# A graph layer, a mixer and merged experts on one core: the head written out step by step, the weight merge shared with TensorE, the last norm divided anew

## The chip, the cores and the metric

The kernel runs on one core of a Trainium2 chip. The core has four engines that compute, TensorE (PE), VectorE (DVE), ScalarE (ACT) and GpSimd (POOL), and SyncE (SP), whose queue issues the DMAs here. Each engine works through its own queue in order and waits on semaphores for what others produce. The metric is device time in microseconds of one execution. Times that are read from the trace count from the first instruction of the span.

## The reference, cut to what matters

```python
xn = layernorm(x)                                  # x: 1250 x 512
h = prelu(xn @ lin_W.T + lin_b, lin_a)             # the linear layer of the head
for l in range(2):                                 # graph convolution
    h = h + segment_sum(h[src], dst)               # 41250 edges, sorted by dst
    h = prelu(h @ W1[l].T + b1[l], a[l]) @ W2[l].T + b2[l]
    h = relu(batchnorm(h))
x = x + h + mixer(xn)                              # linear attention, layer norm
y = layernorm(x)
g = (relu(y @ gfc1.T + b) @ gfc2.T + b2).mean(0)   # 8 gates, one set for all rows
W1m = W1 + sum(g[e] * tv_W1[e]);  b1m = b1 + g @ tv_b1
W2m = W2 + sum(g[e] * tv_W2[e]);  b2m = b2 + g @ tv_b2
out = x + norm(y + relu(y @ W1m.T + b1m) @ W2m.T + b2m)
```

## The kernel before

Nodes lie in ten tiles of 128 rows (the last has 98), features in four tiles of 128. A float32 product over four feature tiles appears in the trace as eight PE records.

**The head** (lines 694 to 864). For each row tile `x_first` takes mean and variance on VectorE and the root on ScalarE, `x_second` the inverse on VectorE and the normalised rows on ScalarE, `x_third` turns the rows by PE into features and copies them out of PSUM on ScalarE (line 607). `lin(c0, cn, f)` makes the product of one feature tile for `cn` nodes (PE, line 576), two Relu sides on ScalarE (612, 613), and their sum on VectorE (614). The node parts are 256, 256, 384 and 354 wide. Before the first rows arrive PE turns the identity 22 times (line 723). The calls stand under `given(engines={PE, DVE, Activation})`: on these three engines the order of the queue is the order of the program, up to `head.close()` at line 861. The last part of the linear layer, and all up to the second layer's end, is ordered by the framework's own planner; from line 1200 on the program's order holds again.

**The graph as a matrix.** Between these calls the lines 745 to 794 make, from the sorted edges, the first destination of each of the 81 blocks of 512 edges (`ends`, `span`, `base`), and keys (`s_hi`, `s_lo`, `key`). `weave(us)` then lets blocks into the work at a rate of 0.70 per microsecond given: for a block, one-hot rows `oh_s` and `oh_k` on VectorE (832, 834), or, for every third block, `oh_s` on ScalarE (817, 818); four PE products (849); and an add into `adj` (851). `drain(keep=2)` leaves two blocks between making and counting. 10 of the 81 blocks are let in during the linear layer, the others in the key stage (line 884) and after it. The first graph product (line 981) needs all.

**The merge** (lines 1300 to 1366). When the gates are known (line 1297), eight expert weights are added to `m1` (4 chunks of 128x256) and `m2` (2 chunks of 128x512). On VectorE: `m1` chunks 0, 1, 2 and `m2` chunk 0, each as a chain of eight multiply-adds in a PSUM bank. By ScalarE scaling in place and GpSimd adding: `m1` chunk 3 and `m2` chunk 1. `joined(c)` multiplies chunk `c` into six PSUM banks (`parts`: two feature tiles by three node parts, line 1325), and after chunk 3 ScalarE takes the Relu. The bias row `b2` is one product (1334) before chunk 0; it is added to the rows `xn2` in advance, tiles 0 to 4 on VectorE, 5 to 9 on GpSimd.

**The end** (lines 1370 to 1442). For each row tile: product (1374), sum with `xn2` on VectorE (1384, 1388), the norm, and the store. A `NEAR` tile has its last steps on VectorE (1413 to 1416), any other one on ScalarE and GpSimd (1424 to 1429). Tiles in `BY_SCALAR` have their variance taken on ScalarE, and their last steps three tiles later.

Of the kernel before, what the change touches and what calls it, by code (L numbers as in the profile page):

```python
# [9 lines left out]
F32 = mybir.dt.float32  # L10
# [515 lines left out]
def usual_block(  # L526
# [75 lines left out]
    def to_features(dst, t, src, n):  # L602

        pt = bank()
        for c in range(DT):
            nc.tensor.transpose(pt[:, c * P:c * P + n], src[:, c * P:(c + 1) * P], ident[0:n, 0:n])
        nc.scalar.copy(dst[:, :, t * P:t * P + n], pt.rearrange("p (c n) -> p c n", c=DT)[:, :, 0:n])  # L607

    def prelu(dst, ps, cn, bias, slope):

        u = tmp.tile([P, CHUNKS[0][1]], F32, tag="xt", bufs=4, name="u")
        nc.scalar.activation(dst, ps[:, :cn], AF.Relu, bias=v(*bias))  # L612
        nc.scalar.activation(u[:, :cn], ps[:, :cn], AF.Relu, bias=minus(*bias), scale=-1.0)  # L613
        nc.vector.scalar_tensor_tensor(dst, u[:, :cn], minus(*slope), dst, op0=ALU.mult, op1=ALU.add)  # L614
# [79 lines left out]
    x_live = {}  # L694

    def x_first(t):
        x_live[t] = spread(x_in[0:rows(t), t, :], rows(t))

    def x_second(t):
        n = rows(t)  # L700
        mv, rs = x_live.pop(t)
        inverse(mv, rs, n)
        normal(xn[0:n, t, :], x_in[0:n, t, :], rs, n)

    def x_third(t):
        to_features(xn_t, t, xn[0:rows(t), t, :], rows(t))

    h_t = large("C", [P, DT, N], name="h_t")

    def lin(c0, cn, f):  # L710
        ps = bank()
        gemm(ps, cn, lambda c: lw[:, c, f * P:(f + 1) * P], lambda c: xn_t[:, c, c0:c0 + cn])
        prelu(h_t[:, f, c0:c0 + cn], ps, cn, ("lin_b", f), ("lin_a", f))
# [3 lines left out]
    head = ExitStack()  # L717
    head.enter_context(given(engines={E.PE, E.DVE, E.Activation}))
    idle = bank()

    def stay_warm(n):
        for i in range(n):
            nc.tensor.transpose(idle[:, 0:P], ident, ident)

    stay_warm(22)
    x_first(0)
    x_first(1)
    x_second(0)
    x_second(1)
    x_third(0)  # L730
    x_third(1)
    stay_warm(3)
    x_first(2)
    x_second(2)
    x_first(3)
    x_second(3)
    lin(0, 256, 0)
    x_third(2)
    x_first(4)
    lin(0, 256, 1)  # L740
    x_third(3)
    x_second(4)
    x_first(5)
    lin(0, 256, 2)
    e_d = early.tile([P, NB, J], F32, name="e_d")
    nc.scalar.copy(e_d, edges[:, :, 1, :])
    ends = early.tile([P, 2, NB], F32, name="ends")
    nc.vector.tensor_reduce(ends[:, 0, :], e_d, AX.X, ALU.min)
    real = early.tile([P, NB, J], F32, name="real")
    nc.vector.scalar_tensor_tensor(real, e_d, float(N), e_d, op0=ALU.is_lt, op1=ALU.mult)  # L750
    nc.vector.tensor_reduce(ends[:, 1, :], real, AX.X, ALU.max)
    x_second(5)
    lin(0, 256, 3)
    x_third(4)
    x_first(6)
    pts = [bank(), bank()]
    lin(256, 256, 0)
    for k in range(2):
        nc.tensor.transpose(pts[k][0:NB, 0:P], ends[:, k, :], ident)
    span = early.tile([NB, 2], F32, name="span")  # L760
    for k, op in ((0, ALU.min), (1, ALU.max)):
        nc.vector.tensor_reduce(span[:, k:k + 1], pts[k][0:NB, 0:P], AX.X, op)
    x_second(6)

    s_hi = early.tile([P, NB, J], I32, name="s_hi")
    nc.vector.tensor_scalar(s_hi, edges[:, :, 0, :], 7, None, op0=ALU.logical_shift_right)
    lin(256, 256, 1)
    x_third(5)
    x_first(7)
    lows, highs = bank(), bank()  # L770
    nc.tensor.transpose(lows[:, 0:NB], span[:, 0:1].to_broadcast([NB, P]), ident[0:NB, 0:NB])
    nc.tensor.transpose(highs[:, 0:NB], span[:, 1:2].to_broadcast([NB, P]), ident[0:NB, 0:NB])
    base = const.tile([P, NB], F32, name="base")
    nc.vector.tensor_scalar(base, lows[:, 0:NB], float(N - W), None, op0=ALU.min)
    base_i = early.tile([1, NB], I32, name="base_i")
    nc.vector.tensor_copy(base_i, base[0:1, :])
    lin(256, 256, 2)
    x_third(6)
    x_second(7)
    low = const.tile([1, 2, NB], F32, name="low")  # L780
    nc.scalar.copy(low[:, 0, :], lows[0:1, 0:NB])
    nc.scalar.copy(low[:, 1, :], highs[0:1, 0:NB])
    key = e_d
    nc.vector.tensor_tensor(key, e_d, base.unsqueeze(2).to_broadcast([P, NB, J]), ALU.subtract)
    nc.vector.tensor_scalar(real, key, float(W), float(BIG), op0=ALU.is_ge, op1=ALU.mult)
    x_first(8)
    lin(256, 256, 3)
    nc.vector.tensor_tensor(key, key, real, ALU.add)
    nc.vector.scalar_tensor_tensor(key, s_hi, float(W), key, op0=ALU.mult, op1=ALU.add)
    x_second(8)  # L790
    x_first(9)
    lin(512, 384, 0)
    s_lo = early.tile([P, NB, J], F32, name="s_lo")
    nc.vector.scalar_tensor_tensor(s_lo, s_hi, -float(P), edges[:, :, 0, :], op0=ALU.mult, op1=ALU.add)
    x_third(7)
    x_second(9)
# [13 lines left out]

    held, state = [], {"block": 0, "due": 0.0, "at": []}

    def source_rows(b, oh_s):

        off = hot.tile([P, J, P], F16, bufs=2, name="off")
        for j in range(J):
            nc.scalar.activation(off[:, j, :], count16[:, 0:P], AF.Abs, bias=s_lo[:, b, j:j + 1], scale=-1.0)
        nc.scalar.activation(oh_s, off, AF.Relu, bias=1.0, scale=-1.0)  # L818

    def weave(us, keep=2):  # L820

        state["due"] += us * PACE
        while state["block"] < min(NB, state["due"]):
            b = state["block"]
            state["block"] += 1
            oh_s = hot.tile([P, J, P], F16, name="oh_s")
            oh_k = hot.tile([P, J, NT * W], F16, name="oh_k")
            if b % 3 == 1 and b > 3:
                source_rows(b, oh_s)
            for j in range(J):  # L830
                if b % 3 != 1 or b <= 3:
                    nc.vector.tensor_scalar(oh_s[:, j, :], count16[:, 0:P], s_lo[:, b, j:j + 1], None,  # L832
                                            op0=ALU.is_equal)
                nc.vector.tensor_scalar(oh_k[:, j, :], count16, key[:, b, j:j + 1], None, op0=ALU.is_equal)  # L834
            held.append((b, oh_s, oh_k))
            drain(keep)

    def drain(keep):
        while len(held) > keep:
            b, oh_s, oh_k = held.pop(0)  # L840
            if b % 16 == 0:
                k = min(16, NB - b)
                _, state["at"] = nc.values_load_multi_w_load_instructions(
                    base_i[0:1, b:b + k], engines=[mybir.EngineType.DVE], min_val=0, max_val=N - W,
                    skip_runtime_bounds_check_because="both ends are taken from 0 to N - W",
                )
            ps = bank()
            for j in range(J):
                nc.tensor.matmul(ps[:, 0:NT * W], oh_s[:, j, :], oh_k[:, j, :], start=(j == 0), stop=(j == J - 1))  # L849
            at = ds(state["at"][b % 16], W)  # L850
            nc.vector.tensor_tensor(adj_r[:, :, at], adj[:, :, at],  # L851
                                    ps[:, 0:NT * W].rearrange("p (s d) -> p s d", s=NT), ALU.add)

    PACE = 0.70

    for f in range(1, DT):
        weave(1.4)
        lin(512, 384, f)
        if f < 3:
            x_third(f + 7)  # L860
    head.close()
    for f in range(DT):
        weave(2.4)
        lin(896, 354, f)
# [433 lines left out]
    nc.scalar.activation(gate9[0:NE, :], pg9[0:NE, 0:P], AF.Identity, bias=g2bc, scale=1.0 / N)  # L1298
# [4 lines left out]
    parts = [(f, b, bank()) for f in range(FT) for b in range(len(CHUNKS))]  # L1303
# [5 lines left out]
    def merge(acc, dst, srcs, at, alone=False):  # L1309

        for e in range(0 if alone else 1, NE):
            nc.vector.scalar_tensor_tensor(dst[at] if alone and e == NE - 1 else acc, srcs[e][at], gate[:, e:e + 1],
                                           dst[at] if alone and e == 0 else acc, op0=ALU.mult, op1=ALU.add)
        if not alone:
            nc.vector.tensor_tensor(dst[at], acc, dst[at], ALU.add)

    def merge_far(dst, srcs, at):
        for e in range(NE):
            scaled(srcs[e][at], e, srcs[e][at])
            nc.gpsimd.tensor_tensor(dst[at], dst[at], srcs[e][at], ALU.add)  # L1320
# [190 lines left out]
```

## Time and profile before

| | |
|---|---|
| times of three runs | 571.64, 571.74, 572.16 us; median 571.74 |
| the profiled execution | 570.89 us, its span 569.1 us |
| mean granted PE clock | 0.989 |
| busy PE, DVE, ACT, POOL | 545.6, 324.7, 244.2, 75.3 us |
| first linear product starts | 8.41 us |
| first key product starts | 57.33 us |
| first graph product starts | 203.22 us |
| products of the gate layer end | 515.37 us |
| gates known | 517.22 us |
| joined products | 521.52 to 540.40 us |
| output products | 540.40 to 557.73 us |
| VectorE's last instruction ends | 563.17 us |

Busy time is the time in which an engine executes an instruction; a wait isn't in it. A record of the trace gives an instruction's start and duration. Where instructions of a kind follow one another without a wait, the distance of their starts is less than the duration, because the next begins while the last is finishing; a sum over many uses that distance, a wait for a result uses the duration. The profiled execution is one of several, and 0.85 us below the median.

### The profile page before, as it was taken

To read this page: it belongs to the slowest core of one execution; us is meant where nothing else is said; L and a number is where in the kernel's file an instruction comes from. 1 tells how busy PE (TensorE), PEld (TensorE's weight loads), DVE (VectorE), ACT (ScalarE), POOL (GpSimd) and SP (SyncE) were. 2 spreads that over 40 slices of the span, in tenths; PEclk is the share of its full clock that TensorE was granted. 3 is DMA by queue.
4 is the path that set the end of the run, shared out by engine and by line. 5 is a ranking of instruction groups with operands and counts; after the bars stand their busy time and mean duration, and the time that the engine had idled before them with its cause. 6 is when DMAs were issued, how large, how long until landed. Compare 5 with 4: busy or idle time off the path is not lost. (4 is left out here: it accounts for less than half of the span.)

```text
span 569.1 us, 6958 instructions
## 1 busy us (share of the span) xinstructions
PE 545.6 (96%) x2367; PEld 368.1 (65%) x2367; DVE 324.7 (57%) x1097; ACT 244.2 (43%) x539; POOL 75.3 (13%) x73
## 2 busy tenths in 40 slices
PE   8799999999999999999999999999999999997992
PEld 7655568799955567777754454449995556864540
DVE  4579999976899724444425534121112248726885
ACT  6676664554354212223333344112333446726453
POOL 8200000000000000000004331000000001204972
PEclk9999999999999999999999999999999999997997
DMA  9500200020021010000311102000008320402014
GB/s 282 184 1 1 74 2 1 1 75 2 1 94 56 0 75 0 1 1 2 104 44 37 37 1 74 0 0 1 2 0 282 124 74 1 147 1 75 0 41 146
DMA packets 19285, 29.10 MB, mean 51 GB/s; under 512 B 1529, under 2 KB 8185, under 8 KB 19240
## 3 DMA queue, kind: packets, MB, share of 16 engines
q1 hardware_dynamic: 19096, 28.52, 14.8%
q8 instruction: 20, 0.33, 0.2%
q14 instruction: 25, 0.20, 0.1%
q10 hardware_dynamic: 144, 0.05, 0.0%
HBM read 26.01 MB, written 2.56 MB: 50 GB/s over the span
## 5 line engine op out<-in xcount | busy, mean ns | idle before, releaser
L981 PE MATMUL bank<-adj,y_h 128*128 128x416 f32 (+1 forms) x240 | 86.5, 361 | 1.1 <-DVE adj L851 1.1
L834 DVE TENSOR_SCALAR oh_k<-count,e_d 128x240 f16<-128x240 f16 x324 | 84.4, 281 | 0.0
L981 PE MATMUL bank<-adj,y_l 128*128 128x416 f32 (+1 forms) x240 | 84.4, 352 | 0.0
L1083 POOL TENSOR_TENSOR m<-m,ls_bc 128x512 f32<-128x512 f32 (+1 forms) x10 | 12.7, 1270 | 447.6 <-ACT m L600 447.6
L968 PE MATMUL bank<-w,h_t 128*128 128x512 f32 (+1 forms) x160 | 70.4, 592 | 0.0
L576 PE MATMUL bank<-z_t,w 128*128 128x416 f32 (+1 forms) x192 | 68.9, 513 | 0.0
L576 PEld LDWEIGHTS bank<-z_t,w 128*128 128x128 f32 x192 | 36.1, 189 | 31.8 <-issue 30.0
L832 DVE TENSOR_SCALAR oh_s<-count,s_lo 128x128 f16<-128x128 f16 x220 | 55.8, 254 | 0.0
L968 PEld LDWEIGHTS bank<-w,h_t 128*128 128x128 f32 (+1 forms) x160 | 29.4, 188 | 34.8 <-issue 34.5
L614 DVE SCALAR_TENSOR_TENSOR z_t<-u,m_sb,z_t 128x416 f32<-128x416 f32 (+1 forms) x24 | 15.7, 652 | 59.8 <-ACT u L613 59.8
L981 PEld LDWEIGHTS bank<-adj,y_h 128*128 128x128 f32 x240 | 45.1, 188 | 2.6 <-issue 2.1
L981 PEld LDWEIGHTS bank<-adj,y_l 128*128 128x128 f32 x240 | 45.2, 188 | 1.2 <-issue 0.7
L849 PE MATMUL bank<-oh_k,oh_s 128*128 128x240 f16 x324 | 41.8, 266 | 1.6 <-ACT oh_s L818 1.2
L849 PEld LDWEIGHTS <-oh_s 128*128 128x128 f16 x324 | 31.6, 98 | 16.4 <-issue 5.3
L612 ACT ACTIVATE z_t<-bank,v_sb 128x416 f32<-128x416 f32 (+1 forms) x24 | 14.7, 610 | 61.4 <-PE bank L981 61.4
L851 DVE TENSOR_TENSOR adj<-adj,bank 128x240 f32 x81 | 32.7, 404 | 13.9 <-PE bank L849 12.5
L995 DVE BATCH_NORM_STATS2 bst<-bank 128x6 f32<-128x416 f32 (+1 forms) x24 | 14.4, 600 | 42.9 <-ACT h_t L994 42.9
L917 PE MATMUL bank<-kk,xn 128*128 128x128 f32 (+1 forms) x320 | 38.4, 275 | 0.0
L576 PE MATMUL bank<-xn_t,lw 128*128 128x256 f32 (+2 forms) x128 | 36.6, 428 | 0.8 <-ACT xn_t L607 0.8
L917 PEld LDWEIGHTS bank<-kk,xn 128*128 128x128 f32 (+1 forms) x320 | 37.0, 192 | 0.1
L1064 PE MATMUL bank<-mixer,q_t 128*128 128x512 f32 (+1 forms) x80 | 36.3, 592 | 0.0
L576 PE MATMUL bank<-xn_t,gw 128*128 128x256 f32 (+2 forms) x128 | 35.3, 427 | 0.9 <-ACT xn_t L607 0.9
(172 smaller groups left out, 797.3 us busy)
## 6 DMA issues: line engine op xcount, KB each, us to landing
t<-in_tv_w SPq DMA_DIRECT2D x12, 512.0 KB, 7.6
w<-in_conv_w SPq DMA_DIRECT2D x4, 1024.0 KB, 5.4
x_in<-in_x SPq DMA_DIRECT2D x9, 256.0 KB, 4.7
xt<-in_x SPq DMA_DIRECT2D x9, 256.0 KB, 4.2
out<-m SPq DMA_DIRECT2D x9, 256.0 KB, 2.7
rest<-in_tv_w SPq DMA_DIRECT2D x4, 512.0 KB, 5.1
lw<-in_lin_w SPq DMA_DIRECT2D x4, 256.0 KB, 5.1
wk<-in_w_qkv SPq DMA_DIRECT2D x1, 1024.0 KB, 7.1
```

Of the source, the lines that this page charges most:

```text
L576: nc.tensor.matmul(ps[:, :cn], lhs(c), rhs(c), start=(c == 0), stop=(c == k - 1))
L612: nc.scalar.activation(dst, ps[:, :cn], AF.Relu, bias=v(*bias))
L614: nc.vector.scalar_tensor_tensor(dst, u[:, :cn], minus(*slope), dst, op0=ALU.mult, op1=ALU.add)
L832: nc.vector.tensor_scalar(oh_s[:, j, :], count16[:, 0:P], s_lo[:, b, j:j + 1], None, op0=ALU.is_equal)
L834: nc.vector.tensor_scalar(oh_k[:, j, :], count16, key[:, b, j:j + 1], None, op0=ALU.is_equal)
L849: nc.tensor.matmul(ps[:, 0:NT * W], oh_s[:, j, :], oh_k[:, j, :], start=(j == 0), stop=(j == J - 1))
L851: nc.vector.tensor_tensor(adj_r[:, :, at], adj[:, :, at], ps[:, 0:NT * W].rearrange("p (s d) -> p s d", s=NT), ALU.add)
L917: nc.tensor.matmul(ps[:, c * P:(c + 1) * P], xn[0:n, t, c * P:(c + 1) * P], k_nodes(f)[0:n, t, :], start=(t == 0), stop=(t == NT - 1))
L968: nc.tensor.matmul(ps[:n], h_t[:, c, t * P:t * P + n], w1[:, c, :], start=(c == 0), stop=(c == DT - 1))
L981: nc.tensor.matmul(ps[:, :cn], y[0:n, s, f * P:(f + 1) * P], adj_r[0:n, s, c0:c0 + cn], start=(s == 0 and y is ys[0]), stop=(s == NT - 1 a ...
L995: nc.vector.bn_stats(st[:, b, :], ps[:, :cn])
L1064: nc.tensor.matmul(ps[:n], q_t[:, h, t * P:t * P + n], mixer[:, h, :], start=(h == 0), stop=(h == DT - 1))
```

## The change

Three places change. What each engine computes for the result is the same sum in another division.

1. **The head.** Each call is split into single steps of one engine, and the string `HEAD_ORDER` gives their order to the end of the linear layer; the digits are the tile, or part and feature tile. The node parts are 128, 256, 384 and 482. The copy of tile 0 is on VectorE. ScalarE makes one-hot rows only for blocks after the ninth. All ten blocks of the head are also counted and added within it.
2. **The merge.** In chunk 0 of `m1` the left 128 columns are summed by PE, with identities scaled by the gates as one operand; the right 128 stay on VectorE. Chunk 1 goes to ScalarE and GpSimd, chunks 2 and 3 to VectorE as one piece of 512 columns. The bias row's product and `gate9` come later. `joined` takes its parts in a given list; the last two parts of chunk 3 come before output tile 5. Row tiles 0 to 5 get their bias on VectorE.
3. **The last norm.** Tile 5 leaves `NEAR` and `BY_SCALAR`; the last steps of a `BY_SCALAR` tile come two tiles later instead of three.

```diff
+    HEAD_ORDER = """
+        s0 s1 q0 r0 q1 s2 n0 r1 t0 q2 s3 n1 c0 t1 q3 r3 m00 c1 r2 n2 m01 u00 n3 t2 j00 m02 s4 u01 c2 j01
+        t3 s5 u02 m03 ed j02 q5 m10 ends u03 q4 c3 j03 tends s6 u10 m11 r5 q6 span n5 r4 hi n4 tspan s8
+        m12 u11 base low key q8 t5 r8 u12 t4 put m13 c5 j12 c4 j10 n8 r6 lo m20 n6 s9 u13 s7 q9 j13 q7
+        j11 t6 r7 u20 m21 r9 b0 c6 n7 j20 n9 b1 d0 u21 m22 j21 b2 t7 u22 m23 b3 c7 b4 d1 u23 t9 j22 t8
+        c9 d2 j23 c8 d3 a0 b5 m30 b6 b7 d4 u30 m31 j30 a3 a4 a2 b8 d5 u31 m32 b9 j31 a5 d6 a1 u32 m33 a6
+        j32 d7 u33 d8 a7 d9 a8 j33 a9
+    """
+    PARTS = ((0, 128), (128, 256), (384, 384), (768, 482))
+    COPIED_BY_VECTOR = (0,)
...
+    def one_hot_rows(b):
...
+        by_scalar = b % 3 == 1 and b > 9
...
+    def counts(b):
+        _, oh_s, oh_k = held.pop(0)
+        live["block", b] = ps = bank()
+        for j in range(J):
+            nc.tensor.matmul(ps[:, 0:NT * W], oh_s[:, j, :], oh_k[:, j, :], start=(j == 0), stop=(j == J - 1))
...
+    STEPS = {
+        "s": x_stats, "q": x_root, "r": lambda t: inverse(x_mv[:, t, :], x_rs[:, t, :], rows(t)), "n": x_normal,
+        "t": x_turn, "c": x_copy, "m": lin_product, "u": lin_sides, "j": lin_join,
+        "ed": lambda: nc.scalar.copy(e_d, edges[:, :, 1, :]), "ends": ends_of_blocks, "tends": turn_ends,
+        "span": reduce_ends, "tspan": spread_ends, "base": bases, "low": lowest, "hi": source_high,
+        "lo": source_low, "key": keys_in_band, "put": keys, "b": one_hot_rows, "d": counts, "a": add_counts,
+    }
+    with given(engines={E.PE, E.DVE, E.Activation}):
...
+        for step in HEAD_ORDER.split():
+            name = step.rstrip("0123456789")
+            STEPS[name](*(int(i) for i in step[len(name):]))
...
+    state["due"] = float(state["block"])
...
-    nc.scalar.activation(gate9[0:NE, :], pg9[0:NE, 0:P], AF.Identity, bias=g2bc, scale=1.0 / N)
...
+    gated = [tmp.tile([P, 2, P], F32, tag="xt", bufs=4, name="gated") for _ in range(NE // 2)]
+    one = [flat(t, 1, 2) for t in t1s]
+    two = [flat(t, 2, 4) for t in t1s]
+    for e in (0, 1, 2, 4, 5, 6):
+        nc.vector.tensor_scalar(gated[e // 2][:, e % 2, :], ident, gate[:, e:e + 1], None, op0=ALU.mult)
+    scaled(gated[1][:, 1, :], 3, ident)
+    merge_far(flat(m1, 1, 2), one, [0])
+    scaled(gated[3][:, 1, :], 7, ident)
+    merge_far(flat(m1, 1, 2), one, [1, 2])
+    nc.tensor.matmul(sums[1][:, 0:P], ident, m1[:, 0, 0:P], start=True, stop=False)
     for e in range(NE):
+        nc.tensor.matmul(sums[1][:, 0:P], gated[e // 2][:, e % 2, :], t1s[e][:, 0, 0:P],
+                         start=False, stop=(e == NE - 1))
+    acc = sums[0][:, 0:FF - P]
+    for e in range(NE):
+        nc.vector.scalar_tensor_tensor(m1[:, 0, P:FF] if e == NE - 1 else acc, t1s[e][:, 0, P:FF], gate[:, e:e + 1],
+                                       m1[:, 0, P:FF] if e == 0 else acc, op0=ALU.mult, op1=ALU.add)
+    nc.scalar.copy(m1[:, 0, 0:P], sums[1][:, 0:P])
+    joined(0, sorted(parts, key=lambda p: p[0]))
+    merge_far(flat(m1, 1, 2), one, [3])
+    scaled(sums[1], 0, two[0])
+    merge_far(flat(m1, 1, 2), one, range(4, NE))
     nc.vector.tensor_reduce(mb1, mb, AX.X, ALU.add)
+    merge(sums[1], flat(m1, 2, 4), two)
...
+    nc.scalar.activation(gate9[0:NE, :], pg9[0:NE, 0:P], AF.Identity, bias=g2bc, scale=1.0 / N)
...
+    far2 = [t[:, 1, :] for t in t2s]
+    merge_far(m2[:, 1, :], far2, range(2))
+    joined(1, parts)
+    nc.tensor.matmul(sums[0], gate9, r9[:, 0, :], start=True, stop=True)
+    nc.scalar.copy(b2, sums[0])
+    shifted(0)
+    scaled(sums[1], 0, t2s[0][:, 0, :])
+    merge(sums[1], m2[:, 0, :], [t[:, 0, :] for t in t2s])
+    merge_far(m2[:, 1, :], far2, range(2, NE))
+    joined(2, parts)
+    joined(3, parts[0:4])
+    for t in range(1, NT):
+        shifted(t)
...
-    NEAR, BY_SCALAR = (4, 5, 7, 8, 9), (5, 7, 8, 9)
+    NEAR, BY_SCALAR = (4, 7, 8, 9), (7, 8, 9)
...
-    for t in range(NT + 3):
+    for t in range(NT + 2):
         for u in NEAR:
-            if u == t - (3 if u in BY_SCALAR else 1):
+            if u == t - (2 if u in BY_SCALAR else 1):
                 out_near(u)
+        if t == 5:
+            joined(3, parts[4:])
         if t < NT:
             out_product(t)
             out_sum(t)
```

The steps are: `s` statistics, `q` root, `r` inverse, `n` normalise, `t` turn, `c` copy, `m` product, `u` the two Relu sides, `j` their join, `b` one-hot rows of a block, `d` its counts, `a` the add into `adj`; the named ones are the edge preparation. `merge_far(dst, srcs, es)` now takes the experts as a list: ScalarE scales, GpSimd adds. `shifted(t)` adds the bias row to tile `t`, on VectorE for `t < 6`, else on GpSimd.

## The prediction

> **What bounds the kernel.** I read the page first, then PE's waits, then a table by stretches, then the timeline of the two places that the change touches. The page says how long, which engine, and at what clock:
>
> ```profile
> span 569.1 us, 6958 instructions
> PE 545.6 (96%) x2367; PEld 368.1 (65%) x2367; DVE 324.7 (57%) x1097; ACT 244.2 (43%) x539; POOL 75.3 (13%) x73
> PEclk9999999999999999999999999999999999997997
> ```
>
> TensorE is the bound: 96% busy, at full clock but for two slices near the end. So a gain is idle PE time taken out, or slow-clock time. Where it idled, from PE's waits (waiter, releaser, us in total, times, longest):
>
> ```profile
> PE bank L1325 <- DVE m L1312: 2.5, 1, 2.5
> PE bank L771 <- DVE span L762: 2.4, 1, 2.4
> PE bank L576 <- ACT xn_t L607: 1.7, 3, 0.9
> PE bank L849 <- ACT oh_s L818: 1.2, 1, 1.2
> PE bank L981 <- DVE adj L851: 1.1, 1, 1.1
> ```
>
> The first lies in the weight merge, the others but for the last mostly in the head. By stretches (start:end, length, busy us and instructions of PE, PEld, DVE, ACT, POOL; PE clock; DMA share; GB/s):
>
> ```profile
> 8.41:20.00 11.59, 11.06 (x57) 9.34 (x58) 6.34 (x20) 7.46 (x17) 8.84 (x11) 1.00 1.06 348
> 20.00:40.00 20.00, 17.03 (x77) 11.57 (x76) 12.65 (x44) 13.67 (x33) 0.00 (x0) 1.00 0.08 29
> 40.00:57.33 17.33, 15.78 (x74) 9.71 (x72) 16.04 (x75) 11.79 (x30) 0.00 (x0) 1.00 0.00 1
> 57.33:202.13 144.80, 144.80 (x862) 104.37 (x861) 125.23 (x594) 66.95 (x171) 0.00 (x0) 1.00 0.09 30
> 515.20:521.52 6.32, 3.34 (x19) 1.78 (x17) 4.34 (x11) 3.87 (x10) 1.70 (x4) 0.78 0.47 167
> 521.52:540.40 18.88, 18.88 (x49) 10.15 (x50) 16.42 (x30) 10.86 (x20) 17.94 (x18) 0.89 0.00 1
> ```
>
> From 57.33, the first key product (call it T), PE has no gap until 202. So time saved before T is saved at 202, if VectorE still feeds the one-hot blocks as early relative to T. Last, the timeline of the merge and the end (start, us, engine, line):
>
> ```profile
> 521.52 19.04 PE L1325 MATMUL bank<-xn_t,m 128*128 128x418 f32 x48 [2.54 <-DVE m L1312]
> 540.40 17.33 PE L1374 MATMUL bank<-m,a_t 128*128 128x512 f32 x40
> 562.42 0.75 DVE L1416 SCALAR_TENSOR_TENSOR m<-bank,rs,x_sb 98x512 f32<-98x512 f32 x1
> ```
>
> The end is VectorE's: it finishes 5.4 us after the last product, then a store.
>
> **The head: PE's work.** A product is eight PE records. From the timeline these start 0.216 us apart at 256 columns, 0.322 at 384, 0.297 at 354, 0.350 at 418, 0.429 at 512, 0.112 at 128. At 482 no row exists; between 418 and 512 it is 0.404. Before: 4 x 8 x (0.216 + 0.216 + 0.322 + 0.297) = 33.6 us. After (128, 256, 384, 482): 4 x 8 x (0.112 + 0.216 + 0.322 + 0.404) = 33.7. No work is saved. Besides, from the first product on: eight row turns of 0.435 = 3.5, the block ends some 0.8, ten blocks of counts at 0.41 = 4.1 (before 9.75 blocks by T). Sum after: 42.2. Before, T - 8.41 = 48.9 for 41.8 of work: 7.1 us of holes.
>
> **The head: does PE run dry?** I walk the written order, each engine taking its steps in sequence at the spacing of their rows: statistics 0.83, root 0.21 (result 0.30), inverse 0.27, normalise 0.71 (result 0.82), copy 0.48 (0.58), the two Relu sides 2 x 0.26, 0.36, 0.46, 0.54 (by width; the first and last along the line through the others), join 0.27, 0.40, 0.54, 0.64, one block's one-hot rows 1.42 on VectorE, count add 0.31; 0.04 from engine to engine. The same walk over the old order gives its first product at 8.38 (trace 8.41), the turned ends at 24.23 (24.28), the first product of 384 at 28.98 (29.19). It errs by 0.2.
>
> The new start is later. VectorE: s0 to 4.33, s1 to 5.16, r0 to 5.43, then s2, which waits until 6.67 for its rows; r1, now behind s2, ends 7.77 (before: 5.9). s3 waits for the fourth tile (issued 3.16, longest landing of this group 5.1: 8.26) and holds the copy c0 behind it; that copy on VectorE lies between ScalarE's 0.58 and the 0.70 of L1388, taken 0.65. First product: 9.77, a loss of 1.4. From there the walk finds every operand before PE asks: the nearest are tends by 0.22, t2 by 0.39, t3 by 0.49, m20 by 0.57, tspan by 0.64; only m30 waits, 0.13. Blocks 4 and 7, moved to VectorE (8 x 0.16 = 1.3 more), are hidden: from d1 on, one-hot rows stand ready 3 us or more before PE (without that cover, 1.3 us). So T = 9.77 + 42.2 + 0.1 = 52.1: **-5.2**. VectorE or ScalarE 10% slower throughout gives at most 52.6; best case, -5.6. No DMA is added or moved; the next weight load (wo) waits for the last linear product as before and is needed some 45 us later.
>
> Is it kept? VectorE leaves the head at 53.2, T + 1.1, and has block 11's rows at T + 3.35; before at T + 3.41 (60.74). As early relative to T, so kept. Reserve is thin: VectorE is busy 42.4 of the 42.7 us to 100.
>
> **The merge.** Gates are ready at 517.22. New on VectorE: six scalings of a 128x128 identity, no such row; between 0.13 and 0.25 (L832 in f16 goes at 0.16, L785 with 324 f32 columns at 0.25), taken 0.17: 1.0. Then eight merges of 128 columns; 256 go at 0.52, 512 at 0.78, so 0.39 (bounds 0.30 to 0.52): 3.1. The right half is ready at 521.4, no sooner than the whole before. The left half: eighteen PE records at 0.11 follow the scalings, done 519.5; a copy on ScalarE, behind five scalings, to 519.9. Joined products start at 520.0 instead of 521.52: -1.5. GpSimd now owes chunk 1: eight adds at 0.79 from 518.1, done 524.7, while PE is done with chunk 0 at 524.2: waits 0.6. (Six parts, two sums and the unread gate product are nine banks for eight; ScalarE reads that product at 522.9, before the sixth part asks at 523.5.) Chunk 1 ends 528.9. Then comes the bias row's product, which lay in idle time before and now costs 0.86: 529.8.
>
> Here a new wait forms. The copy b2 on ScalarE waits for that product, and behind it in the same queue stand the scaling that opens VectorE's merge of m2 (530.5 to 531.2; 7 x 0.78 + 0.6 follow, to 537.5) and six scalings for GpSimd (first done 531.9; six adds of 1.31, to 539.9). GpSimd idles 4.6 us meanwhile, VectorE 2.5 in front of its first shift. PE, with only four of the six last parts taken before the output, is done at 536.8, waits 0.7 for one half of m2 and 1.6 for the other. First output product done at 540.8, nine more of 1.71 and the two deferred parts (1.4): **557.6**, where it was 557.7. The early start is given back.
>
> **The last norm.** Tile 5 goes from VectorE (sum 0.7 + 1.52) to GpSimd (sum and statistics 1.56; 2.57 there, done 560.2): VectorE saves 0.66. On SP's queue the store of tile 7 now stands behind that of tile 6 (560.2), the last one behind neither. But tile 7's last steps stand before tile 9's sum and wait for ScalarE: 557.4 to 558.9, then the sum, then tile 8, then tile 9: end 562.6 against 563.17. The walk on the old order gives 562.9, so I take **-0.3** (from -1.5, if adds are shorter, to +2.2, below).
>
> [...] The row 515.20:521.52 has a clock of 0.78, and 521.52:540.40 has 0.89: 2 us were lost because PE warmed up again. In the new order PE gets full-width products from 517.6 on, longest pause 0.6, so I take full clock. [...] By the row it is less sure: the clock fell although PE shows records in half of that stretch. If it falls again, the merge ends 1.1 to 2.5 us later. [...]
>
> **Sum.** -5.2 - 0.3 = -5.5. Against the profiled execution, span 569.1 and 570.89 with what lies around it, 565.4. The median shown is 571.74, 0.85 above that execution; the same difference gives **566.2**.
>
> **Rivals.** (1) As above: 62%, 565.2 to 567.2. (2) The clock falls once in the merge or the head, +1.1 to +2.5: 568.0; the fall at the same place before speaks for it, the new full-width products against it; 18%. (3) The head's gain is partly waited away at the blocks, since VectorE has no reserve to 100: half lost, 568.8, all lost, 571.4; equal lead over T speaks against it; 9%. (4) The m2 chain is shorter than walked and PE never waits there: PE ends 2.3 sooner, VectorE, then the bound, some 1.6 sooner than before: 564.9; 5%. (5) Slower: the rest is planned anew behind the written head, and the one-hot rows come late at each of the 39 places where blocks are woven in. At 0.2 us each that is 7.8: 574.0; it beats the gain from 0.14 us each. No PE gap in 145 us speaks against it; 6%. That the order doesn't do what it says is in (3).
>
> The range 564.6 to 569.6 takes (1), (2), (4) and the better part of (3). A change within 0.2% (1.1 us) can't be told from none: faster 0.90, same 0.04, slower 0.06.
>
> **What would show it.** First linear product near 9.8, first key product near 52.1, no PE wait between; first joined product near 520.0 and bias product near 529 (both 5.2 earlier by then); GpSimd idle some 4 us before its third m2 add; PE waiting some 2 us before the output; VectorE's end 5 us after PE's. I am wrong if T is past 54, if PE waits for one-hot rows after T, or if the clock is half in the joined products.

## The result and the profile after

| | before | after | ratio (95%) |
|---|---|---|---|
| median, us | 571.69 (571.21 to 572.16, 4 runs) | 566.61 (565.33 to 568.56, 4 runs) | 0.9916 (0.9899 to 0.9933) |
| profiled execution, us (span) | 570.89 (569.1) | 568.56 (566.1) | |

The forecast was 566.2, in a range of 564.6 to 569.6. The profiled execution of the changed kernel is the longest of its four, so its trace shows a loss that the median does not have. From its page, the first lines, the busy time of each engine and the granted clock in 40 slices:

```profile
span 566.1 us, 6992 instructions
PE 546.7 (97%) x2385; PEld 368.6 (65%) x2385; DVE 325.4 (57%) x1104; ACT 238.8 (42%) x529; POOL 77.0 (14%) x74
PEclk8999999999999999999999999999999999999997
```

TensorE is still the bound. The lower clock has gone from the end of the span, where the merge stands, to its first slice, where the head starts. The waits of PE (waiter, releaser, us in total, times, longest):

```profile
PE bank L1421 <- POOL m L1351: 1.4, 1, 1.4
PE bank L576 <- DVE xn_t L609: 1.3, 1, 1.3
PE bank L1012 <- DVE adj L861: 1.1, 1, 1.1
PE bank L1421 <- ACT a_t L1359: 0.4, 1, 0.4
PE bank L1356 <- ACT m L1383: 0.4, 1, 0.4
```

The 2.5 on `m` in the merge and the 2.4 on `span` are gone. In their place stand a wait of 1.4 for GpSimd before the output (the line 1421 was 1374), and one of 1.3 before the first linear product. By stretches (start:end, length, busy us and instructions of PE, PEld, DVE, ACT, POOL; PE clock; DMA share; GB/s):

```profile
10.34:20.00 9.66, 9.66 (x58) 9.22 (x59) 6.53 (x24) 7.45 (x20) 7.76 (x11) 0.83 1.05 364
20.00:40.00 20.00, 20.00 (x96) 13.88 (x95) 17.72 (x75) 15.89 (x39) 0.00 (x0) 1.00 0.07 24
40.00:53.98 13.98, 13.98 (x53) 7.30 (x52) 11.67 (x52) 6.47 (x13) 0.00 (x0) 1.00 0.01 1
53.98:198.60 144.62, 144.62 (x862) 104.27 (x860) 124.35 (x588) 65.49 (x167) 0.00 (x0) 1.00 0.10 30
516.65:534.58 17.93, 17.18 (x46) 8.42 (x47) 14.39 (x24) 11.08 (x21) 12.09 (x14) 1.00 0.00 1
```

From the first linear product to 198.6 PE has no gap; before, it had 3 us of idle time between 20 and 40 alone. The clock is 0.83 in the first stretch and 1.00 in the joined products, where it was 0.89. As key times (T is the first key product, line 576):

| us from the span's start | before | after | after, run again |
|---|---|---|---|
| first linear product | 8.41 | 10.34 | 10.12 |
| T | 57.33 | 53.98 | 52.18 |
| first graph product, less T | 145.89 | 145.72 | 145.71 |
| VectorE's end, less T | 505.84 | 505.99 | 506.01 |

So the gain is made before T, it is kept to the end, and everything behind T together brings nothing. The third column is the run `e5_changed_again` below. From the first linear product to T it takes 42.06 us where the second column takes 43.64: those 1.58 us are the clock in the head, 0.50 from 10.29 to 13.70.

### The profile page after: what moved, and what is told of

It reads as the page before. It is cut to its first block, busy times and chain, and to the rows that moved or that the text cites. A ratio compares the mean times of both kernels' runs of the same rounds, so it can differ in the third digit from the quotient of the medians.

```text
span 566.1 us, 6992 instructions
## 1 busy us (share of the span) xinstructions
PE 546.7 (97%) x2385; PEld 368.6 (65%) x2385; DVE 325.4 (57%) x1104; ACT 238.8 (42%) x529; POOL 77.0 (14%) x74
## 5 line engine op out<-in xcount | busy, mean ns | idle before, releaser
L850 PE MATMUL bank<-oh_k,oh_s 128*128 128x240 f16 x324 | 40.6, 266 | 0.0
L576 PE MATMUL bank<-xn_t,lw 128*128 128x128 f32 (+3 forms) x128 | 37.7, 446 | 1.3 <-DVE xn_t L609 1.3
```

The lines of the kernel that those rows point to most:

```text
L576: nc.tensor.matmul(ps[:, :cn], lhs(c), rhs(c), start=(c == 0), stop=(c == k - 1))
```

## The experiments

All runs gave a time beside the kernel before on the same chip, whose medians were 571.24, 571.99 and 571.73 us in the three groups.

### One part alone

`e1_head_only` is the kernel before with the new head, merge and last norm as they were. `e2_tail_only` is the kernel before with the new merge and last norm, and the old head. Their edits are the first part of the diff above, and the second and third.

> The new head with the old merge and the old last norm. Theory A (the gain is the head's alone, carried whole to the end): 571.7 - 5.2 = 566.5 where the clock stays full in the head, 568.2 where it falls there for one window; the last VectorE instruction 5 us or 3.5 us earlier than the old 563.17. Theory B (head and merge share the gain, since the profiled span fell by only 3.0): about 568.5 to 570 at full clock in the head.

> The old head with the new merge and the new last norm. Theory A: no change that can be told, 571.4 to 572.4; joined products start 1.5 us sooner, PE waits some 1.4 us for GpSimd's half of m2 and ends its output products no sooner than 557.7. Theory B: 569 to 570.

Measured: the head alone 566.78 us, ratio 0.9925 (0.9907 to 0.9943); the merge and the norm alone 572.84, ratio 1.0019 (1.0009 to 1.003), which is 1.1 us slower. In the trace of the head alone T is at 51.84, and VectorE ends 505.30 later; with the tail alone T is at 57.73 and VectorE ends 506.18 later. The tail alone was expected at 571.4 to 572.4 and came out slower than that. What follows: the whole gain is the head's. The new merge has full clock (1.00 from 516.65 to 534.58 in the changed kernel; a mean of 0.994 over the tail's profiled execution) where with the old one it was 0.50 for 6.83 us in the kernel before (518.69 to 525.52) and for 3.42 in the head's run (515.71 to 519.13), and still it ends no sooner.

### The start of the head, and its clock

In the profiled execution after, PE's timeline up to the first linear product (start, us, engine, line, operation, tiles, count, idle time before it and its releaser):

```profile
6.88 0.66 PE L605 MATMUL bank<-ident,xn 128*128 128x128 f32 x4 [0.33 <-ACT xn L600]
7.38 0.49 PE L893 MATMUL bank<-ident 128*128 128x128 f32 x3
8.39 0.66 PE L605 MATMUL bank<-ident,xn 128*128 128x128 f32 x4 [0.53 <-ACT xn L600]
10.34 2.08 PE L576 MATMUL bank<-xn_t,lw 128*128 128x128 f32 x8 [1.28 <-DVE xn_t L609]
```

PE has eleven turns between 6.88 and 10.29, and from 10.29 to 13.70 its clock is 0.50. T is then 1.8 later than in the next run of the same kernel, 0.2 of it because the first product starts later. `e5_changed_again` is that next run; `e3_head_filled` gives PE more turns of the identity there:

```diff
-            if step == "t0":
-                for i in range(3):
-                    nc.tensor.transpose(idle[:, 0:P], ident, ident)
+            for i in range({"t0": 8, "t1": 11}.get(step, 0)):
+                nc.tensor.transpose(idle[:, 0:P], ident, ident)
```

and `e9_no_turns` takes the three turns behind `t0` away:

```diff
-            if step == "t0":
-                for i in range(3):
-                    nc.tensor.transpose(idle[:, 0:P], ident, ident)
```

> The changed kernel with 16 more turns of the identity on PE in the two pauses before its first linear product (8 instead of 3 after the first tile's turn, 11 after the second's). Theory A (in the profiled execution the clock fell because PE was mostly idle between 6.9 and 10.3): full clock in the head in every execution, first key product near 52.2 instead of 53.98, median 565 to 566, and the executions closer together than 565.3 to 568.6. [...]

> The changed kernel once more, beside the next three on the same chip. Median 565.5 to 568, single executions spread over 3 us where those of the kernel before spread over 1 to 2. First linear product 1.57 us after the landing of the fourth row tile, whatever that is.

> The changed kernel without the three turns of the identity behind the first tile's turn, so that PE has only the row turns before its first linear product. [...]

Measured: filled 566.86 (566.15 to 569.02), mean clock 0.992 to 0.995 in all six executions, T at 53.05; the changed kernel again 565.98 (565.43 to 567.57, where a spread of 3 was expected), T at 52.18; without the three turns 566.11 (565.62 to 571.95). Only the profiled execution shows where its clock fell; of the others the mean clock alone is known. Profiled executions that kept the clock in the head and in the merge have a mean of 0.992 to 0.995, the two that lost it in the head 0.991 and 0.990, so a mean under 0.992 is taken for a fall.

The half clock of the head lasts 3.41 us in the changed kernel (10.29 to 13.70) and 3.42 in `e4_bias_early` (9.12 to 12.54), that of the old merge 6.83 in the kernel before (518.69 to 525.52). The 3.41 us before the fall in the changed kernel, and the stretch of the half clock, in the columns shown above:

```profile
6.88:10.29 3.41, 1.64 (x11) 1.17 (x11) 2.00 (x8) 1.60 (x4) 3.41 (x1) 1.00 1.09 325
10.29:13.70 3.41, 3.36 (x15) 3.37 (x16) 1.04 (x6) 2.28 (x5) 3.41 (x1) 0.50 1.05 374
```

of the same kernel run again, two stretches as long, the second with its first linear product in it:

```profile
5.69:9.10 3.41, 2.14 (x16) 1.43 (x14) 1.78 (x7) 2.12 (x4) 3.41 (x1) 1.00 1.03 310
9.10:12.51 3.41, 2.39 (x21) 2.39 (x22) 1.91 (x9) 2.64 (x6) 3.41 (x1) 1.00 1.07 362
```

and of the kernel without the three turns, two likewise:

```profile
4.71:8.13 3.42, 1.67 (x13) 1.19 (x11) 2.32 (x10) 2.14 (x5) 3.42 (x2) 1.00 1.01 320
8.13:11.54 3.41, 2.10 (x16) 1.86 (x17) 1.91 (x7) 1.97 (x5) 3.41 (x1) 1.00 1.09 342
```

The first stretch of each holds turns and nothing else. After 2.14 us of them the clock was 1.00, after 1.64 it was 0.50; the kernel without the three turns had 1.00 after 1.67, nearly as little. What decides between these executions is not shown. Without the turns the median, 566.11, is within 0.5 us of the changed kernel's 566.61 and 565.98, and six of the nine executions took 565.6 to 566.2. Two were long, 568.74 and 571.95, at clocks of 0.986 and 0.985; no trace shows where they lost it. Filling kept the clock in all six executions by their means (0.992 to 0.995), but it bought no time: T is at 53.05, 0.9 later than in the run of the changed kernel that kept its clock, and all of that is there at the first linear product (10.99 against 10.12). Nor did it narrow the spread, as was expected: 566.15 to 569.02, with a mean clock of 0.993 in the longest. So the clock is not the only source of the spread.

Why does the first product start so late? VectorE's timeline in the changed kernel shows it:

```profile
7.07 0.18 DVE L739 BATCH_NORM_AGGREGATE x_mv<-st 128x2 f32<-128x6 f32 x1
7.17 0.13 DVE L595 RECIPROCAL x_rs<-x_rs 128x1 f32<-128x1 f32 x1
8.80 0.69 DVE L738 BATCH_NORM_STATS2 st<-x_in 128x6 f32<-128x512 f32 x1 [1.30 <-DMA x_in<-in_x]
9.53 0.18 DVE L739 BATCH_NORM_AGGREGATE x_mv<-st 128x2 f32<-128x6 f32 x1
9.62 0.66 DVE L609 COPY xn_t<-bank 128x512 f32<-128x512 f32 x1
```

The inverse for tile 1 (7.17) waits behind the statistics of tile 2, and the copy `c0` (9.62), for which PE waits, behind those of tile 3, which wait 1.30 us for a DMA. The statistics start when the tile has landed. In the changed kernel, its repeat, `e1_head_only`, `e3_head_filled` and `e4_bias_early` alike the first product starts 1.54 us after that start, which moved between 8.25 and 9.45. `e6_start_reordered` puts `r1` before `s2`, `c0` before `s3`, and the other steps of tile 3 later:

```diff
-        s0 s1 q0 r0 q1 s2 n0 r1 t0 q2 s3 n1 c0 t1 q3 r3 m00 c1 r2 n2 m01 u00 n3 t2 j00 m02 s4 u01 c2 j01
-        t3 s5 u02 m03 ed j02 q5 m10 ends u03 q4 c3 j03 tends s6 u10 m11 r5 q6 span n5 r4 hi n4 tspan s8
+        s0 s1 q0 r0 q1 r1 s2 n0 n1 t0 q2 c0 t1 r2 c1 n2 m00 s3 m01 u00 t2 j00 m02 u01 c2 q3 j01 r3 m03 ed n3
+        u02 s4 j02 ends m10 q4 u03 t3 s5 q5 c3 j03 tends s6 u10 m11 r5 q6 span n5 r4 hi n4 tspan s8
```

> The changed kernel with the first steps in another order: r1 before s2, c0 before s3, and the steps of the fourth tile later. Theory A (r1 behind s2 and c0 behind s3 tie the start to the landing of the third and fourth row tiles, and that alone makes the head vary and its clock fall): first linear product at 8.2 to 8.8, no more than 0.1 us from tile 1's copy, not tied to the fourth tile; no fall of the clock in the head; first key product at 51.5 to 52.1; median 0.8 to 1.8 us under the changed kernel's on this chip. Theory B (the spread comes from elsewhere): first key product as before within 0.5 us, same median.

Measured: 565.67 us (565.52 to 565.93), ratio 0.9895 (0.9881 to 0.991). In its VectorE timeline the copy no longer stands behind the wait:

```profile
6.50 0.69 DVE L738 BATCH_NORM_STATS2 st<-x_in 128x6 f32<-128x512 f32 x1
7.22 0.18 DVE L739 BATCH_NORM_AGGREGATE x_mv<-st 128x2 f32<-128x6 f32 x1
7.49 0.69 DVE L609 COPY xn_t<-bank 128x512 f32<-128x512 f32 x1
8.81 0.69 DVE L738 BATCH_NORM_STATS2 st<-x_in 128x6 f32<-128x512 f32 x1 [0.36 <-DMA x_in<-in_x]
```

The first product starts at 8.24 though tile 3 lands no earlier (8.81), and T is at 51.58. The start 1.9 us earlier brings only 0.6 at T. PE's waits between the two show what takes the rest:

```profile
PE bank L778 <- DVE ends L773: 0.4, 1, 0.4
PE bank L787 <- DVE span L782: 0.3, 1, 0.3
```

PE now runs into the edge preparation, whose turns the prediction had found ready by only 0.22 and 0.64 us. By the distances of starts these two places cost about 1.3 us more than in the repeat of the changed kernel. The median moves by 0.3, less than the spread of the changed kernel, where 0.8 to 1.8 was expected. What changed with the order is the spread: four executions within 0.4 us. Its two descendants below that change nothing else in the head's start, `e8_start_and_bias` and `e10_blocks_by_scalar`, are close too (0.7 and 0.2 us), and none of these 13 executions has a mean clock under 0.992; of the 21 executions of the changed kernel, its repeat, `e4_bias_early` and `e7_old_last_norm`, eight have. It is no guarantee: two of the six executions of `e11_vector_late`, which has the same start, are at 0.991.

### The bias row's product

The prediction named one new wait in the tail: `b2` is copied by ScalarE only when its product is done, and that product stands behind chunk 1 on PE. `e4_bias_early` moves the two lines up:

```diff
     merge_far(m2[:, 1, :], far2, range(2))
-    joined(1, parts)
     nc.tensor.matmul(sums[0], gate9, r9[:, 0, :], start=True, stop=True)
     nc.scalar.copy(b2, sums[0])
+    joined(1, parts)
```

> The changed kernel with the bias row's product and its copy put before the products of chunk 1 instead of behind them. Theory A (the copy that waits for this product holds back the scalings of m2, so PE waits for GpSimd before the output): bias product some 0.4 us after the end of chunk 0's products, GpSimd's third add of m2 some 4 us sooner, no wait of PE longer than 0.5 us before the output products, PE's end 2 to 3 us sooner relative to the gates, 1.5 to 2.5 us off the median. Theory B (GpSimd is the limit whatever the order): PE still waits over 1 us for it, time unchanged within 0.5 us.

Measured: 564.22 us (562.82 to 566.67), ratio 0.9875 (0.9853 to 0.9896). In its profiled execution the clock fell in the head too, to 0.50 from 9.12 to 12.54. VectorE ends 503.28 after T instead of 505.99. The timelines of PE, ScalarE and GpSimd around the wait in the changed kernel:

```profile
525.87 1.12 PE L1404 MATMUL bank<-r,gate 9*128 9x512 f32 x2
527.03 0.58 ACT L1405 COPY b<-bank 128x512 f32<-128x512 f32 x1 [6.36 <-PE bank L1404]
528.98 5.32 POOL L1351 TENSOR_TENSOR m<-m,rest 128x512 f32<-128x512 f32 x4 [4.84 <-ACT rest L1337]
...
537.05 7.99 PE L1421 MATMUL bank<-m,a_t 128*128 128x512 f32 x18 [1.37 <-POOL m L1351]
```

and with the product moved up:

```profile
520.45 1.12 PE L1403 MATMUL bank<-r,gate 9*128 9x512 f32 x2
521.60 0.58 ACT L1404 COPY b<-bank 128x512 f32<-128x512 f32 x1 [1.53 <-PE bank L1403]
525.64 5.35 POOL L1351 TENSOR_TENSOR m<-m,rest 128x512 f32<-128x512 f32 x4 [2.09 <-ACT rest L1337]
...
532.80 8.95 PE L1421 MATMUL bank<-m,a_t 128*128 128x512 f32 x20
```

The same product starts 5.4 us earlier (4.8 counted from T), GpSimd idles 2.09 instead of 4.84 (its third add was expected 4 us sooner), and PE no longer waits before the output. This confirms the wait and gives its price: 2.7 us in the trace.

`e8_start_and_bias` puts both edits together.

> The reordered start and the early bias product together. Theory A (they are independent, each on the path): the gains add, 562.5 to 563.5 on a chip where the kernel before takes 571.2 to 571.7; first key product at 51.5 to 52.1, VectorE's end 503.3 us after it. Theory B (the blocks' supply eats the earlier key stage): VectorE's end more than 504.3 us after it.

Measured: 563.04 us (562.82 to 563.52), ratio 0.9849 (0.9836 to 0.9862). T is at 51.61, and VectorE ends 503.38 later. The gains add as expected: 2.9 less than the changed kernel's repeat on the same chip, nearly all of it the bias product's, and this version is faster than both kernels. Its page:

```profile
span 561.0 us, 6991 instructions
PE 544.3 (97%) x2385; PEld 366.7 (65%) x2385; DVE 325.7 (58%) x1104; ACT 238.5 (43%) x529; POOL 76.7 (14%) x74
PEclk9999999999999999999999999999999999999997
```

### The last norm

`e7_old_last_norm` is the changed kernel with the old division of the last norm:

```diff
-    NEAR, BY_SCALAR = (4, 7, 8, 9), (7, 8, 9)
+    NEAR, BY_SCALAR = (4, 5, 7, 8, 9), (5, 7, 8, 9)
...
-    for t in range(NT + 2):
+    for t in range(NT + 3):
...
-            if u == t - (2 if u in BY_SCALAR else 1):
+            if u == t - (3 if u in BY_SCALAR else 1):
```

> The changed kernel with the old division of the last norm (tiles 4, 5, 7, 8, 9 near, late steps three tiles behind). Theory A (the new division saves what the walk says): 0.4 us slower than the changed kernel, VectorE's end 5.5 us after PE's instead of 4.95. Theory B (it saves the whole 0.75 us of tile 5 or more): 0.8 to 1.5 slower. Theory C (it costs): faster.

Measured: 567.17 us (565.99 to 568.46) against 565.98 of the changed kernel in the same group. VectorE ends 5.44 after PE with the old division and 4.95 with the new one, so the new one saves 0.49. The difference of the medians, 1.2, is larger because the mean clock was 0.991 in three of its six executions (567.72 to 568.46); the median can't give the size.

### VectorE's reserve

Two kernels ask whether the head's gain hangs on VectorE's lead over the blocks. Both start from `e6_start_reordered`. `e10_blocks_by_scalar` gives blocks 4 and 7 back to ScalarE:

```diff
-        by_scalar = b % 3 == 1 and b > 9
+        by_scalar = b % 3 == 1 and b > 3
```

and `e11_vector_late` adds four sums, which nothing reads, at the head's end, some 2.4 us of VectorE:

```diff
+        late_by = tmp.tile([P, D], F32, tag="xt", bufs=4, name="late_by")
+        for i in range(4):
+            nc.vector.tensor_tensor(late_by, x_in[:, i, :], x_in[:, i + 1, :], ALU.add)
```

> The reordered start, with the one-hot rows of blocks 4 and 7 made by ScalarE again. Theory A (in the head VectorE's 1.3 us for them are hidden): first key product at 51.5 to 51.7 and the same time within 0.4 us. Theory B (they are on the path): 0.5 to 1.3 us faster.

> The reordered start, with four sums of 128x512 on VectorE at the end of the head, whose result nothing reads: some 2.5 us more work there, so that VectorE starts on the key stage's blocks later. Theory A (VectorE has no reserve up to 100 us: lateness at the first key product is paid one for one): first key product unchanged at 51.6, first graph product 1.5 to 2.5 us later than 197.3, time up by as much. Theory B (the blocks' place among the products gives way): first graph product within 0.4 us of 197.3, time the same.

Measured: 566.13 us (566.07 to 566.24) with the blocks given back, against 565.67: no gain, so the 1.3 us that they take on VectorE are hidden. Its T was expected at 51.5 to 51.7 and is at 52.24: the first product comes 0.3 later, and PE waits 0.2 for a copy on ScalarE, which now has the blocks. With the four sums 567.27 (566.85 to 569.33). In that trace T is at 52.06, and the first graph product comes 146.99 after T instead of 145.71. Between them stands a wait that no other version has:

```profile
PE bank L850 <- DVE oh_k L843: 0.6, 2, 0.3
```

About half of the 2.4 us is paid, between the two expectations, and half of that is this wait for one-hot rows: the lead covers some delay, but not all. The rest of the 1.3 is not traced; the planner behind the head may lay the blocks anew.

## Why the prediction held, and where it did not

**The head: PE's work** was right. The sum said 42.2 us from the first linear product (its terms add to 42.1), with the one wait 42.3; `e1_head_only` and the changed kernel run again show 42.05 and 42.06. **The head: does PE run dry?** gave T at 52.1, and 51.84 and 52.18 were measured. The first product was given at 9.77, with the loss put down to tile 3's landing and `c0` behind it; it came at 9.79 to 10.34, and at 10.99 in `e3_head_filled`, tied to that landing. What the step left out is that this term moves between executions, as the landing does: here by 1.2 us. That the lead is kept was right: the first graph product follows T after 145.72, before after 145.89, and `e11_vector_late` shows that the reserve is thin, though not nothing. That moving blocks 4 and 7 costs nothing is confirmed by `e10_blocks_by_scalar`.

**The clock** was right for the merge: 1.00 in the joined products, 516.65 to 534.58. The prediction's 2 us for the old merge is an estimate from the clocks 0.78 and 0.89; a warming up of PE is not shown, only that the clock was 0.50 from 518.69 to 525.52 and 1.00 behind it. For the head, T = 52.1 has no loss by the clock in it. The profiled execution shows 53.98, with 0.50 from 10.29 to 13.70, and the run again 52.18, with 1.00 from 5.69 to 12.51. PE's busy time ahead of the products does not explain it: after 3.41 us with turns alone the clock stayed at 1.00 with 2.14, 1.67 and, in `e3_head_filled`, 2.71 us busy, and was 0.50 with 1.64 and, in `e4_bias_early`, 1.48, and the last section has a stretch with 1.48 after which it stayed. Why it falls is not shown. Rival (2) happened in the head, by the mean clocks in one execution of four, and it cost 1.58 us there, within the 1.1 to 2.5 given.

**The merge** named the right mechanism and mis-sized its terms. The forecast had the joined products start 2.78 us after the gates; they started 2.96 after, a gain of 1.34 on the old order instead of 1.5. The new wait then took it back, as was said: GpSimd idle 4.84 (forecast 4.6), PE waiting 1.37 for GpSimd's half of `m2` and 0.39 for the Relus (forecast 2.3 for the two halves of `m2`). Two sums in its walk are 0.2 to 0.3 more than their terms: eight adds of 0.79 from 518.1 end at 524.4, not 524.7, and PE waited 0.36 there instead of 0.6; VectorE's chain of `m2` adds to 537.3, not 537.5. The step that failed is "First output product done at 540.8, nine more of 1.71 and the two deferred parts (1.4): **557.6**": from the gates that is 40.4 us, and 41.3 were measured. The 0.95 are 0.18 in the start, 0.32 in chunks 0 and 1, 0.14 up to the end of the first output product and 0.31 in what follows it. VectorE ends 4.95 after PE, forecast 5.0. So in place of **-0.3** the tail brings +0.15 in the trace, counted from T, and +1.1 by the ratio when it stands alone. With the product moved up (`e4_bias_early`) the same tail gains 2.6, from T. With the new head, both tails end within the spread (566.78 and 566.61).

**The last norm** was right: 0.44 less between PE's end and VectorE's end in the prediction's walk, 0.49 measured.

**The sum** was -5.5. The changed kernel run again, whose clock did not fall, gives by profiled executions 570.89 - 566.09 = 4.8: 5.15 from the head, less 0.17 in the tail and 0.2 at the span's ends. The two medians differ by 5.1. That the median came within 0.4 of 566.2 is in part luck: the sum put the profiled execution at 565.4, and it was 566.09 with a full clock, 0.7 more; but the 0.85 that was added from the profiled execution to the median is not there in that run, whose median is 565.98.

## What to carry to other kernels

In an order written by hand, look for every short instruction that another engine waits for and that stands behind one waiting for a DMA: here moving two such steps ahead took the start off a landing, 1.9 us earlier, of which 0.6 reached the key products, because the next short steps were then late. A small product whose result opens another engine's queue belongs before the long product, not behind it: two lines moved here were worth 2.7 us, half as much as the whole change. And before an order is judged by one trace, ask whether its bound depends on something that moves between executions; take the same kernel's trace twice.

## What the runs showed of the hardware

With the same program the clock in the head differed between executions: the changed kernel had 0.50 from 10.29 to 13.70 in one and took 43.64 us from its first linear product to T; run again it had 1.00 from 5.69 to 12.51 and took 42.06, 1.58 less. PE was not idle before the clock fell: of the 3.41 us before, it was busy for 1.64 in the changed kernel (6.88 to 10.29), for 1.48 in `e4_bias_early` (5.71 to 9.12) and for 2.96 in the kernel before (515.28 to 518.69). Nor did the clock fall wherever PE was as little busy: it was 1.00 after 1.67 us in `e9_no_turns` (4.71 to 8.13) and after 1.48 in the kernel before (20.35 to 23.76). What makes it fall, no run here shows.

In the old merge a fall of the clock cost much less than the PE time in it. With 3.42 us at 0.50 (`e1_head_only`, 515.71 to 519.13) against 6.83 (the kernel before, 518.69 to 525.52) VectorE's end after T changed by only 0.54 us, 505.30 against 505.84. In the first half of the longer one, from 518.69 to 522.10, PE was busy for 0.87 of 3.41 us and waited 2.54 for VectorE.
